# Seven value matmuls between attention's transposes, and layer 2's start moved by one folding step

## The chip, the cores and the metric

One Trainium2 chip, one core of it. The metric is the device time of one execution of the whole program in microseconds (us), the median of several runs. The kernel before takes 3842.15 us, the median of 3 runs that lie between 3840.6 and 3842.97 us. All arithmetic is in 32-bit floats.

## What is computed

The reference is a chain of four layers on a tensor `x` of 2 images, 512 channels and 32 x 32 positions. Layer 0 is a deformable attention with a position bias made by a small network, and a two-layer MLP behind it. Layer 1 is a depthwise-separable convolution whose result steers a deformable 3 x 3 convolution (9 taps, each a weighted sum of four gathered neighbours) and a gate. The change touches the seams behind layer 1, so layers 2 and 3 are what has to be seen:

```python
# layer 2: linear attention, one map per image (d = 64, N = 1024 positions)
Q, K, V = wq @ xf + bq, wk @ xf + bk, wv @ xf + bv
Qf, Kf = delu(Q).T, delu(K)               # delu(x) = 10*relu(x) + exp(10*min(x, 0))
KV = einsum('bmn,bcn->bmc', Kf, V)
norm = 1.0 / einsum('bnd,bd->bn', Qf, Kf.sum(-1) + 1e-10)
x = x + gamma * einsum('bnd,bdc,bn->bcn', Qf, KV, norm)

# layer 3: group norm (32 groups), 8-head softmax attention, output projection
h = group_norm(x) * scale + bias
q, k, v = split(W_qkv.T @ h + b_qkv)      # per head, 64 channels
attn = softmax(q @ k.T / 8, axis=-1)      # 1024 x 1024 per head
out = x + W_out.T @ (attn @ v) + b_out
```

## The kernel before

The two images go through the layers one behind the other, and the kernel weaves the end of one piece of work into the start of the next. The order of TensorE's instructions is the order in which the Python text emits them (`manual_schedule(engines={PE})`); the other engines' orders are worked out by the framework's scheduler from dependences and emission order. So the text is written as generators: each `yield` ends one small portion of matmuls, and the caller decides which generator gives its next portion.

Two seams matter here.

**Seam one: the folding of the second image and layer 2 of the first (in `layers`, L434 to L467).** The deformable convolution's nine weight taps are first multiplied with the pointwise weights of the image ("folding", `Folded.run`, L1415 on). That is 18 steps, two to a tap, each of four matmuls (L1430) and a copy (L1437) on ScalarE (ACT). The tap's 1 MB of weights is loaded by `load1` on the SyncE (SP) queue: an even tap in one transfer (L416), an odd one in two halves (L421). The loop `for i, _ in enumerate(folding)` adds something behind each folding step. From step 2 on that is one portion of `gate_image` (the gate that ends layer 1 of image 0). When the gate says `"gated"`, in step 10, layer 2 of image 0 can begin: `Linear(net, ctx2, side="right")` issues its loads, `wqk` (0.5 MB), `wv` (1 MB) and a bias row, and `aside` becomes the chain of `linear.run(0, ...)` and the group norm's terms. From step 11 on, `next(aside)` adds one of its portions behind each folding step. The first portion is `pqk` of the first half image (L1647, four matmuls), which needs `wqk` and the gated `x`. What is left of `aside` behind step 17 is taken one portion at a time behind each step of the deformable convolution of image 1 (`Deform.run`, L1508 on: four transposes `pt` L1520, then eight matmuls `po` L1552). When `aside` is done, `Attention` is made and loads its weights.

**Seam two: the end of layer 2 of image 1 and the start of attention (end of `layers`, `layer3`, `Attention.heads`).** The values of image 0, `att.values(0, turn)`, are 8 tiles of 128 positions; each tile is four accumulating matmuls (`pv3`, L1883) in one PSUM bank and one eviction by VectorE (DVE, L1892). A portion is one matmul, so there are 32. `BESIDE` says how many of them go behind each portion of layer 2 of image 1; it sums to 19. The other 13 are emitted at the beginning of `heads` as one block:

```python
ahead = [self.exponentials(*part) for part in logits(*work[0])]
for e in ahead:
    self.divide(*e)
for _ in first:
    pass
```

`heads` then runs 64 steps, half of them for each image. Step `at` works on one pair of heads and 128 query rows. On TensorE it emits the logits of the step that follows (`pl`, L1973), half of the weighting of an earlier pair of steps (`po3`, L1988; there is none in steps 0 and 1, because the first pair is only complete behind step 1), and four groups of four transposes (`pt3`, L2025), `g` = 0 to 3. The maxima of the new logits are DVE's (`m`, L2063), the exponentials ACT's (`e`, L2071), the division DVE's (L2075, L2076). The transposes of group 1 are evicted by DVE (L2034), those of groups 0, 2 and 3 by ACT (L2036), and the exponentials of the second head are held behind the eviction of group 0 (`issue_after`). The tag `pt3` has two PSUM buffers. Behind each group stands the `fill` list, pairs of (attention steps, generator, portions): the portions are spread evenly over four slots to a step. Before, the list begins with image 1's group norm terms and normalization over steps 0 to 3 (10 portions, hardly any TensorE work), image 1's 32 value matmuls over steps 4 to 15, and then its queries and keys. These value matmuls use a bank of their own (`spare`), while the rest of image 0's values take their bank from `turn`, which at that point is `pt3`: `banks["turn"] = att.ps_t, "pt3"`.

Of the kernel before, what the change touches and what calls it, by code (L numbers as in the profile page):

```python
# [3 lines left out]

# [1 line left out]

# [244 lines left out]
def chain(*parts):  # L251
    for part in parts:
        yield from part
# [6 lines left out]
def some(generator, steps):  # L260
    for _ in range(steps):
        next(generator, None)
# [14 lines left out]
def layers(net, out):  # L277
# [12 lines left out]
    with ExitStack() as later:  # L290
# [12 lines left out]
        with ExitStack() as l0a:  # L303
# [9 lines left out]
            first = net.pool(l0a, "cpb_ab", 4)  # L313
# [78 lines left out]
        with ExitStack() as l1:  # L392
            ps_m = net.psum(l1, "l1_m", 3)
            held = net.bank(l1, "l1_held")
            banks["turn"] = net.psum(l1, "l1_y", 2), "turn"
            ps_o = net.psum(l1, "l1_po", 2)

            def bank(name):
                return ps_m.tile([128, 512], F32, name=name, tag="bank")

            def po_bank(name):
                return ps_o.tile([128, 512], F32, name=name, tag="po")

            own1, image1 = ExitStack(), ExitStack()
            acc_a, acc_b = net.pool(own1, "df_acc_a"), net.pool(own1, "df_acc_b")
            tmp = net.pool(own1, "df_tmp", 1)
            f1 = Features(net, 1, own1, dram)

            f1.room = acc_b, "dfacc"

            def load1(k):
                if k % 2 == 0:
                    t = acc_b.tile([128, CC, C], F32, name="dc_w_t", tag="dfacc")
                    nc.sync.dma_start(out=t, in_=net.ins["dc_w"][:, k, :, :])  # L416
                    return [t[:, cc, :] for cc in range(CC)]
                parts = []
                for u in range(2):
                    t = got1.tile([128, 2, C], F32, name="dc_w_t", tag="got")  # L420
                    nc.sync.dma_start(out=t, in_=net.ins["dc_w"][:, k, 2 * u : 2 * u + 2, :])  # L421
                    parts += [t[:, 0, :], t[:, 1, :]]
                return parts

            accs.append(acc_a)
            deform0.buffers(image0, 3, 1, 0, side="right")
            deform0.turn, deform0.po, deform0.on_scalar = turn, po_bank, True
            found = f1.run(own1, bank, held, True)
            for i, _ in enumerate(taken):
                some(found, BOTH[i])  # L430
            image0.close()
            gate = gate_image(net, f0, deform0.acc, tmp, bank)
            for _ in range(2):
                some(found, 2)  # L434
                next(gate)

            next(found)
            folded1 = Folded(net, image1)
            got1 = net.pool(image1, "df_got_w", 2)
            first_w = load1(0)  # L440
            deform1 = Deform(net, f1, folded1, [acc_b, acc_a])
            deform1.on_scalar = True
            deform1.buffers(image1, 4, 2, 2)
            folding = folded1.run(f1, turn, load1, first_w)
            ctx2, aside, att = None, None, None
            next(gate)
            some(found, 3)
            for i, _ in enumerate(folding):
                if i < 6:
                    next(found, None)  # L450
                    next(found, None) if i % 2 else None
                if i == 6:
                    some(found, 99)
                    deform1.fetch()
                if i > 1 and aside is None and next(gate) == "gated":
                    own0.close()
                    ctx2 = ExitStack()
                    linear = Linear(net, ctx2, side="right")
                    linear.open(ctx2, side="right")
                    aside = chain(  # L460
                        linear.run(0, bank, held), group_norm_terms(net, linear.tmp, 0, bank)
                    )
                elif aside is not None:
                    next(aside)
                if i > 8:
                    deform1.prime()

            deform1.free["got"].extend([got1] * 2)
            gate = gate_image(net, f1, deform1.acc, tmp, bank)
            for i, _ in enumerate(deform1.run(turn, po_bank)):  # L470
                if att is None and next(aside, "done") == "done":
                    ctx2.close()
                    att = Attention(net, later, side="right")
                if i in range(22, 34, 2):
                    next(gate)
            image1.close()

            att.open_first(later, side="right")
            for _ in att.normalize(0):
                pass  # L480
            keys = chain(*(att.queries_keys(0, hp, turn) for hp in range(CC)))
            for _ in gate:
                some(keys, 5)
            own1.close()
            with ExitStack() as ctx:
                linear = Linear(net, ctx)
                att.open_values(later, side="right")
                linear.open(ctx)
                some(keys, 12)
                values = att.values(0, turn)  # L490
                for i, _ in enumerate(linear.run(1, bank, held)):
                    some(keys, 2)
                    some(values, BESIDE[i])
                some(keys, 99)
        layer3(net, att, later, values, banks, out)


# [7 lines left out]


BESIDE = (1, 2, 1, 1, 1, 1, 1, 1, 1, 1, 3, 3, 1, 1, 0, 0)


def first_layer(net, pool, feat, p, q):  # L510
# [932 lines left out]
class Deform:  # L1443
# [40 lines left out]
    def sum(self):  # L1484

        nc = self.net.nc
        while self.begun < self.PAIRS and self.free["sum"] and len(self.got) > 1:
            pool, t = self.new("sum", [128, 2, 256])
            for q in range(2):
                c, k = self.parts[2 * self.begun + q]  # L1490
                gpool, g = self.got.popleft()
                for s in range(4):
                    w = self.f.wts[:, c, k, s : s + 1]
                    if s == 0 and self.on_scalar:
                        nc.scalar.activation(t[:, q, :], g[:, 0, :], AF.Copy, scale=w)  # L1495
                    elif s == 0:
                        nc.vector.tensor_scalar(t[:, q, :], g[:, 0, :], w, None, ALU.mult)
                    else:
                        nc.vector.scalar_tensor_tensor(  # L1499
                            t[:, q, :], g[:, s, :], w, t[:, q, :], ALU.mult, ALU.add  # L1500
                        )
                self.free["got"].append(gpool)
            self.sums.append((pool, t))
            self.begun += 1
            self.fetch()
# [576 lines left out]
def layer3(net, att, ctx, values, banks, out):  # L2082


    att.open_heads(ctx)
    ps_f = net.psum(ctx, "l3_fill", 1)

    def spare(name):
        return ps_f.tile([128, 512], F32, name=name, tag="fill")

    first = [(0, hp, s0) for hp in range(CC) for s0 in range(0, HW, 128)]
    second = [
        (1, hp, begin + s0)
        for begin, size in ((0, 512), (512, 256), (768, 256))
        for hp in range(CC)
        for s0 in range(0, size, 128)
    ]

    def output(b, s0, size):
        if (b, s0) == (0, 0):  # L2100
            att.load_out()
        return att.project(b, s0, size, out, spare)

    def late(b, s0, size):
        yield from output(b, s0, size)

    fill = [
        (4, chain(group_norm_terms(net, att.small, 1, spare), att.normalize(1)), 10),
        (12, att.values(1, spare), 32),
        (7, att.queries_keys(1, 0, spare), 16),  # L2110
        (7, att.queries_keys(1, 1, spare), 16),
        (6, att.queries_keys(1, 2, spare), 16),
        (6, att.queries_keys(1, 3, spare), 16),
        (5, late(0, 0, 512), 16),
        (6, late(0, 512, 512), 16),
        (5, late(1, 0, 512), 16),
        (6, late(1, 512, 256), 16),
    ]
    banks["turn"] = att.ps_t, "pt3"
    att.heads(first + second, values, fill)  # L2120
    for _ in att.project(1, 768, 256, out, att.last_bank):
        pass


def program(tc, ins, out, vec_at, cst_at):
    with ExitStack() as ctx:
        net = Net(ctx, tc, ins, vec_at, cst_at)
        layers(net, out)
# [20 lines left out]
```

## Time and profile before

One execution was profiled. Its span is the time between the first and the last instruction seen.

| what | value |
|---|---|
| median of 3 runs | 3842.15 us (3840.6 to 3842.97) |
| the profiled execution's own time | 3841.13 us |
| its span | 3839.4 us |
| TensorE (PE) busy in the span | 3734.6 us (97%) |
| DVE, ACT, POOL busy | 2765.1, 2566.8, 188.2 us |
| mean DMA traffic | 44 GB/s |
| mean TensorE clock granted | 0.99 |
| position of seam one | about 2980 to 3045 us |
| position of seam two | about 3285 to 3450 us |

How to read it: 1.7 us of the execution's own time lie outside the span. TensorE's idle time, 104.8 us, is the difference of the span and its busy time. In a timeline a row is a run of equal instructions; its first number is the start in us from the span's start, its second the length, and what stands in brackets is the idle time of the engine before it and what ended that. A 128x512 matmul in 32-bit floats appears as two records in a timeline, so a folding step or one `pqk` portion is "x8" and one value matmul "x2". In a table of stretches the column `PEclk` is the share of TensorE's clock pulses that was granted.

### The profile page before, as it was taken

The page shows a single profiled execution, that of the slowest core. Times are in us where ns is not written, and L with a number is a line of the kernel's source. Part 1 is how long each engine was busy: PE and PEld are TensorE (multiplying, and loading weights), DVE is VectorE, ACT ScalarE, POOL GpSimd, SP SyncE. Part 2 cuts the span into 40 slices and gives each one's busy share as a digit, 9 for nine tenths or more (in the row PEclk, how much of TensorE's full clock was granted, in tenths as well). Part 3 has the DMA queues.
Part 4 walks back from the last instruction along what each step waited for, and adds up shares of the span by engine and source line. Part 5 has one row for each costly group of instructions (what it writes and reads, how often), then busy time and mean ns, then how long its engine had stood idle before and what let it go on. Part 6 is the DMA issues. An engine that isn't in the chain of part 4 may idle for free. (4 is left out here: it accounts for less than half of the span.)

```text
span 3839.4 us, 59395 instructions
## 1 busy us (share of the span) xinstructions
PE 3734.6 (97%) x25356; PEld 1492.3 (39%) x25356; DVE 2765.1 (72%) x3242; ACT 2566.8 (67%) x2941; POOL 188.2 (5%) x180
## 2 busy tenths in 40 slices
PE   7999999999999999999999899999979999899999
PEld 4532222223222322232233444444434544455555
DVE  6999999999999999999999310510475482566565
ACT  7999999999999999999999211211123243345544
POOL 0000000000000000000000000000252150000000
PEclk9999999999999999999999999999989999999999
DMA  3000000000000000000010000022455471000000
GB/s 111 1 23 23 23 1 23 23 23 12 12 23 23 21 3 23 23 23 1 23 56 29 33 0 1 18 82 77 134 173 187 144 273 48 1 12 1 1 20 25
DMA packets 54459, 168.57 MB, mean 44 GB/s; under 512 B 4804, under 2 KB 10436, under 8 KB 51252
## 3 DMA queue, kind: packets, MB, share of 16 engines
q1 hardware_dynamic: 31556, 83.77, 6.3%
q0 software_dynamic: 21776, 79.14, 6.2%
q8 instruction: 200, 3.28, 0.4%
q10 hardware_dynamic: 864, 1.86, 0.1%
q14 instruction: 63, 0.52, 0.0%
HBM read 156.11 MB, written 8.65 MB: 43 GB/s over the span
## 5 line engine op out<-in xcount | busy, mean ns | idle before, releaser
L888 PE MATMUL ph<-h,w_t 128*32 128x512 f32 x16384 | 1796.8, 593 | 14.0 <-ACT lo L898 6.5
L868 DVE TENSOR_TENSOR h<-ab 128x1024 f32<-128x1024 f32 x1024 | 1206.0, 1219 | 73.2 <-PE ph L888 72.2
L888 PEld LDWEIGHTS ph<-h,w_t 128*32 128x32 f32 x16384 | 548.7, 110 | 1235.5 <-issue 1031.2
L877 ACT ACTIVATE h<-h 128x1024 f32<-128x1024 f32 x832 | 869.6, 1065 | 44.4 <-DVE h L868 40.6
L901 DVE SCALAR_TENSOR_TENSOR hi<-lo,low_w,hi 128x1024 f32<-128x1024 f32 x512 | 655.0, 1279 | 27.4 <-ACT hi L900 26.8
L900 ACT ACTIVATE hi<-ph,size_b,size 128x1024 f32<-128x1024 f32 x512 | 620.5, 1212 | 15.5 <-PE ph L888 10.1
L898 ACT ACTIVATE lo<-ph,vec_t 128x1024 f32<-128x1024 f32 x512 | 571.1, 1116 | 3.8 <-PE ph L888 3.8
L2071 ACT ACTIVATE e<-pl,m 128x1024 f32<-128x1024 f32 x128 | 143.6, 1122 | 228.1 <-DVE m L2063 228.1
L1552 PE MATMUL po<-fold,turned 128*128 128x512 f32 x576 | 269.7, 612 | 3.1 <-DVE dfacc L1560 2.9
L2063 DVE TENSOR_REDUCE m<-pl 128x1 f32<-128x1024 f32 x128 | 150.8, 1220 | 144.4 <-PE pl L1973 144.4
L1120 ACT ACTIVATE h<-ph,vec_t 128x512 f32<-128x512 f32 x64 | 44.0, 687 | 310.9 <-PE ph L1112 310.4
L909 PE MATMUL sim<-hi,w 128*32 128x512 f32 x2048 | 246.1, 592 | 0.6 <-DVE hi L901 0.6
L1112 PE MATMUL ph<-xn,room 128*128 128x512 f32 x512 | 230.2, 593 | 0.0
L1101 PE MATMUL acc<-h,mlp_w_t 128*128 128x512 f32 x512 | 229.8, 592 | 0.0
L1499 DVE SCALAR_TENSOR_TENSOR sum<-got,wts,sum 128x256 f32<-128x256 f32 x432 | 184.4, 479 | 48.1 <-ACT sum L1495 45.7
L1475 POOL DMA_INDIRECT got<-table,idx x144 | 174.0, 1209 | 550.4 <-DVE sum L1499 272.1
L2025 PE MATMUL pt<-cst_t,e 128*128 128x128 f32 x1024 | 148.2, 278 | 6.5 <-ACT aT L2036 3.9
L2025 PEld LDWEIGHTS pt<-cst_t,e 128*128 128x128 f32 x1024 | 117.9, 141 | 93.2 <-issue 61.0
L1552 PEld LDWEIGHTS po<-fold,turned 128*128 128x128 f32 x576 | 107.8, 197 | 114.8 <-issue 109.7
L1101 PEld LDWEIGHTS acc<-h,mlp_w_t 128*128 128x128 f32 x512 | 97.3, 190 | 122.5 <-issue 122.0
L1112 PEld LDWEIGHTS ph<-xn,room 128*128 128x128 f32 x512 | 96.2, 190 | 117.2 <-issue 116.6
L1526 ACT COPY turned<-pt 128x512 f32<-128x512 f32 x72 | 41.9, 582 | 145.9 <-PE pt L1520 145.7
(250 smaller groups left out, 2712.1 us busy)
## 6 DMA issues: line engine op xcount, KB each, us to landing
ab<-feat_d SPq DMA_DIRECT2D x64, 512.0 KB, 3.8
room<-in_dc_w_dram SPq DMA_DIRECT2D x9, 1024.0 KB, 4.7
dc_w_t<-in_dc_w_dram SPq DMA_DIRECT2D x5, 1024.0 KB, 4.8
room<-in_mlp_w_dram SPq DMA_DIRECT2D x1, 4096.0 KB
mlp_w_t<-in_mlp_w_dram SPq DMA_DIRECT2D x1, 4096.0 KB, 13.4
dc_w_t<-in_dc_w_dram SPq DMA_DIRECT2D x8, 512.0 KB, 5.1
w_qkv_t<-in_w_qkv_dram SPq DMA_DIRECT2D x3, 1024.0 KB, 8.9
out_dram<-x_all SPq DMA_DIRECT2D x12, 256.0 KB, 2.0
```

What stands on the lines that cost most here:

```text
L868: nc.vector.tensor_tensor(h1.rearrange("p (y x) -> p y x", x=32), at_x[:, k : k + 1, :].to_broadcast([128, 32, 32]), at_y[:, k, :].unsquee ...
L877: nc.scalar.activation(h1, h1, AF.Relu)
L888: nc.tensor.matmul(ph[32 * t : 32 * t + 32, half(n)], lhsT=w2[:, c0 : c0 + 32], rhs=pair[t // 2][:, half(n)], start=True, stop=True, skip_ ...
L898: nc.scalar.activation(lo, phs[0], AF.Relu, bias=b2_lo)
L900: nc.scalar.activation(hi, phs[1], AF.Relu, bias=size_b, scale=size)
L901: nc.vector.scalar_tensor_tensor(hi, lo, low_w, hi, ALU.mult, ALU.add)
L909: nc.tensor.matmul(sim[32 * t : 32 * t + 32, half(n)], lhsT=w3[:, 30 - j : 62 - j], rhs=sums[t][:, half(n)], start=(j == 0), stop=(j == 30 ...
L1101: nc.tensor.matmul(accs[oc], lhsT=self.w2[:, m, 128 * oc : 128 * oc + 128], rhs=hs[m], start=(m == 0), stop=(m == 15),)
L1112: nc.tensor.matmul(ph, lhsT=self.w1[:, k, 128 * m : 128 * m + 128], rhs=xn[:, k, :], start=(k == 0), stop=(k == CC - 1),)
L1499: nc.vector.scalar_tensor_tensor(t[:, q, :], g[:, s, :], w, t[:, q, :], ALU.mult, ALU.add)
L1552: nc.tensor.matmul(self.out, lhsT=turned[:, at : at + 128], rhs=self.folded.w[k][:, i, :], start=(k == 0 and i == 0), stop=(k == 8 and i = ...
L2025: nc.tensor.transpose(pt[:, 128 * c : 128 * c + 128], e[:, 128 * k : 128 * k + 128], ident)
```

## The change

Two edits. In seam one a single empty portion is put ahead of layer 2 of image 0 (`iter((None,))`), so that its first `pqk` and everything of `aside` behind it is emitted one folding step (later on: one deformable step) later. The loads of `Linear` stay where they are.

In seam two the 13 leftover value matmuls (`LEFT`) are split. `BEHIND` = 6 of them stay in the block ahead of attention's step 0: the last one of tile 4, all four of tile 5, the first one of tile 6. The other 7 become the first entry of `fill`, over steps 0 and 1: none behind group 0 of step 0 and one behind each of the seven groups after it. Image 1's group norm entry thereby moves from steps 0 to 3 to steps 2 to 5, and its 32 value matmuls from 12 steps (4 to 15) to 10 (6 to 15). From step 16 on nothing is changed. The number of instructions is the same.

```diff
+from itertools import islice
...
                     linear.open(ctx2, side="right")
+
                     aside = chain(
+                        iter((None,)),
                         linear.run(0, bank, held), group_norm_terms(net, linear.tmp, 0, bank)
                     )
...
 BESIDE = (1, 2, 1, 1, 1, 1, 1, 1, 1, 1, 3, 3, 1, 1, 0, 0)
+
+
+LEFT = 32 - sum(BESIDE)
+BEHIND = LEFT - 7
...
     fill = [
+        (2, values, LEFT - BEHIND),
         (4, chain(group_norm_terms(net, att.small, 1, spare), att.normalize(1)), 10),
-        (12, att.values(1, spare), 32),
+        (10, att.values(1, spare), 32),
         (7, att.queries_keys(1, 0, spare), 16),
...
-    att.heads(first + second, values, fill)
+    att.heads(first + second, islice(values, BEHIND), fill)
```

## Prediction, made before the changed kernel ran

> **What bounds the kernel now.** I read the page's busy times first, then TensorE's list of waits, then the timeline and short stretches at the two seams.
>
> ```profile
> PE 3734.6 (97%) x25356; PEld 1492.3 (39%) x25356; DVE 2765.1 (72%) x3242; ACT 2566.8 (67%) x2941; POOL 188.2 (5%) x180
> ```
>
> TensorE is the bound, and the change removes none of its work. It can only win idle time, 104.8 us in the whole span, or time at a reduced clock. TensorE's waits, longest first, show how little of that lies at the seams (us in total, times, longest):
>
> ```profile
> PE pv L1883 <- DVE v L1892: 4.3, 5, 2.3
> ...
> PE pt L2025 <- ACT aT L2036: 3.9, 2, 2.0
> PE pqk L1647 <- DMA wqk_t<-in_wqk_dram: 3.8, 1, 3.8
> ...
> PE pt L2025 <- DVE aT L2034: 2.5, 2, 2.1
> ```
>
> Seam one is one wait of 3.8 us. The timeline, and two stretches of it, with the granted clock as the third number from the right:
>
> ```profile
> 2988.91 0.33 SPq L217 DMA_DIRECT2D wqk_t<-in_wqk_dram  x1
> ...
> 2993.52 5.29 PE L1647 MATMUL pqk<-x_all,wqk_t 128*128 128x512 f32 x8 [3.75 <-DMA wqk_t<-in_wqk_dram]
> ...
> 2998.65 3.60 PE L1430 MATMUL pw<-dc_w_t,pw_n_t 128*128 128x512 f32 x8
> ...
> 3002.08 3.60 PE L1647 MATMUL pqk<-x_all,wqk_t 128*128 128x512 f32 x8
> ```
>
> ```profile
> 2989.80:2993.40 3.60, 0.00 (x0) 0.00 (x0) 0.00 (x0) 1.87 (x2) 0.00 (x0) 1.00 0.96 331
> 2993.40:2996.80 3.40, 3.28 (x4) 1.52 (x5) 0.00 (x0) 0.00 (x0) 0.00 (x0) 0.50 0.97 355
> ```
>
> The idle stretch is followed by 3.4 us at half clock: `pqk` takes 5.29 us there and 3.60 the next time. So the wait costs 3.75 + 1.69 = 5.4 us.
>
> Seam two, TensorE alone:
>
> ```profile
> 3300.82 12.12 PE L1883 MATMUL pv<-w_qkv_t,h 128*128 128x512 f32 x24 [2.26 <-DVE v L1892]
> 3312.87 1.99 PE L1973 MATMUL pl<-qk 64*128 64x512 f32 x8
> 3314.79 1.09 PE L2025 MATMUL pt<-cst_t,e 128*128 128x128 f32 x8
> 3317.89 1.10 PE L2025 MATMUL pt<-cst_t,e 128*128 128x128 f32 x8 [2.00 <-ACT aT L2036]
> 3318.91 2.06 PE L1973 MATMUL pl<-qk 64*128 64x512 f32 x8
> 3320.90 1.09 PE L2025 MATMUL pt<-cst_t,e 128*128 128x128 f32 x8
> 3323.92 1.50 PE L2025 MATMUL pt<-cst_t,e 128*128 128x128 f32 x8 [1.93 <-ACT aT L2036]
> ```
>
> Steps 0 and 1 idle 2.00 and 1.93 us each: groups 0 and 1 take both `pt3` buffers, and group 2 waits for ACT's copy of group 0. That copy stands on ACT behind the exponential of new logits, which stands behind their maximum: from the start of `pl` at 3312.87 the maxima start at +2.02, the exponential at +3.28, the copy ends at +4.97. From 3345 on TensorE waits for nothing over 0.6 us.
>
> **Seam one, step by step.** The extra empty portion puts the folding step that is at 2998.65 ahead of the first `pqk`. Its weights (even tap, one 1 MB load) were issued at 2982.05; such loads land in a median of 4.8 us, so they are there by about 2987. TensorE is free at about 2989.6, the step takes 3.44 us beside others (8 records of 0.43), to 2993.05. `wqk`, issued at 2988.91, lands at 2993.38 (4.48 us in the chain of waits), so `pqk` starts at about 2993.5 as before, now at full clock because 0.4 us of idle time are left: to 2996.95. Before, the two were done at 3002.08. **Gain 5.1 us.**
>
> What moves with it: on SP and POOL nothing changes place. The last tap's load waits for the buffer of the folding step, which now ends 8 us sooner, and is used 6 us sooner. Attention's weights are issued one deformable step later than at 3103.81 and first used behind 3186. The second image's deformable convolution starts with one layer-2 portion less ahead of it, so its sums of gathered rows are due sooner. Third pair, the tightest: its sum is complete 4.1 us behind the first transposes now (3031.06, 3035.2), and will be needed 7.8 us behind them. DVE is busy 13 to 20 of every 20 us at 3040 to 3180 and TensorE waits for it nowhere; I take 0, with 2 us as the other end (a wait of the size of the slack at the fourth pair, 3042.3 to 3044.29). Without this cover nothing of the 5.1 would come home.
>
> **Seam two, step by step.** The wait of 2.26 us ahead of tile 5 stays (same maxima ahead of the same eviction). Then 10 instead of 24 records, and step 0 begins 14 x 0.43 = 6.0 us sooner. The point is what tile 6 does: it is begun in the block and finished behind group 3 of step 0, so it holds one `pt3` buffer all through step 0, and tile 7 holds one through step 1. In the changed kernel's emitted order group 1 therefore waits for ACT's copy of group 0, group 2 for DVE's copy of group 1, group 3 for ACT's: **the transposes go through one buffer**. From the start P of `pl`, with the offsets above:
>
> - step 0: `pl` to 1.92, group 0 to 2.47, then idle to 5.01 (copy at 4.97): 2.54 us. Group 1 to 5.56, value matmul to 6.42; DVE, which now divides first (to 5.5), has copied group 1 by about 6.35. Group 2 to 6.97, value to 7.83, group 3 to 8.38, value to 9.24. Three values are 2.58 us, so the rest is 6.66 against 6.04 now: **+0.6**.
> - step 1: one value matmul lies ahead of group 1's wait, idle falls to 1.7 us; 9.24 less four values (3.44) is 5.80, against 6.66 less 0.36 (`pm`, which moves away) less 0.4 (clock) = 5.90: **-0.1**.
>
> The seven matmuls stand nearly all behind the wait and do not fill it. Then image 1's group norm and values come two steps later: steps 2 and 3 have logits, weighting and transposes alone, without fill. Step 2 now is the nearest row: it idles 0.20 and 0.34 us. Two more such steps cost 2 x 0.54 = **+1.1**; the ends are 0 and the 2.11 us of step 3, where normalization stands in DVE's way, so 0 to +4.2. Steps 4 and 5 inherit today's 2 and 3. Steps 6 to 15 have 3.2 values a step instead of 2.7 and are bound by TensorE's work, as now. Sum of seam two: **+1.6**.
>
> **Clock.** Here a row and a rule part. The stretch 3297.15 to 3300.57 has 2.0 us idle and is followed by 3.4 us at 0.50; so are the ones with 1.93 and 2.11; the one with 1.77 of its 3.45 us idle (3314.2 to 3317.65) is not. The Trainium skill, "TensorE: Matmul & The Clock Gate", Part 1, says that half clock follows a whole idle window of about 3.4 us, and under "HAM oscillation" it advises contiguous matmuls to stay warm, which speaks against breaking up a block. By the rule as written none of the gaps of seam two costs clock and the sum is +1.6 on either side. By the rows each gap of 1.9 or more can cost 1.7: now three do (2.26, 1.93, 2.11), and afterwards 2.26, 2.54 and 2.11 can, while 1.7 lies below. I follow the rows: three for three, 0, with one spell (1.7) either way, since the windows run freely and the seam moves against them.
>
> **Sum.** -5.1 + 1.6 = -3.5. Against the profiled execution's own 3841.13 that is 3837.6. The median of the runs is 1.0 above it, so I forecast **3838.6**, its own range 3835.5 to 3842.
>
> **Rivals.**
> - *The values fill the gaps.* If the other buffer comes free, or the copies come sooner, both step gaps (3.93) vanish and one clock spell with them (1.7): 3842.15 - 5.1 - 3.9 - 1.7 + 1.1 = **3832.5**. For it: 7 x 0.86 us of work lie in just these steps. Against it: the buffer's holder and the chain of maximum, exponential, copy, which the values do not shorten. 0.17.
> - *The single buffer costs more than seam one brings (the slower side).* Every group 1 to 3 of both steps waits behind the exponentials (about 4.4 a step, 8.7 for 3.9 now: +4.8), the emptier stretches bring two more half-clock spells (+3.4), the two unfilled steps cost step 3's price (+4.2): +12.4 - 5.1 = +7.3, **3849.5**. It decides from +5.1 in seam two on. For it: 2.54 of a window of 3.4 idle in step 0. Against it: a value matmul of 0.86 covers each later copy of 0.6 to 0.7. 0.16.
> - *Seam one gives nothing.* `wqk` lands no sooner and the 5 us come back as a wait for gathered sums: 3842.15 + 1.6 = **3843.7**. For it: DMA is 0.94 busy at 3100 to 3120. Against it: no wait there now. 0.11.
>
> **Chances.** Forecast 0.56. 0.2% is 7.7 us, about what a measurement of this kernel can tell from no change: faster is below 3834.5 (nearly all of the first rival, a little of the forecast, 0.18), slower above 3849.8 (half of the second rival and a trace of the third, 0.09), within it 0.73. The range 3831 to 3847 holds the forecast, the first and third rival and the lower part of the second.
>
> **What would show it.** In the changed profile: `pqk` at about 3.6 us with at most 0.5 us of wait (right), a wait for a sum (L1499) behind 3020 (seam one given back). In step 0 a gap of about 2.5 us between group 0 and group 1 put down to ACT's copy (right); no gap over 1 us in steps 0 and 1 would prove the single buffer wrong. Gaps over 1 us in steps 2 and 3 would mean that I priced the unfilled steps too low.

## The result, and the profile after

The changed kernel takes 3837.68 us, the median of 12 runs (3833.46 to 3840.63); beside them the kernel before takes 3842.16 us (12 runs, 3839.74 to 3846.77). The two medians lie 4.5 us apart. The recorded ratio, which is not simply that of the medians, is 0.9984 with a 95% interval of 0.9977 to 0.9991: 6.1 us less, between 3.5 and 8.8. Taken again in two later groups of runs, the ratio was 0.9987 (0.9978 to 0.9995) and 0.9984 (0.9975 to 0.9993). So the gain is real in that none of the three intervals reaches 1. All three middle values are below the 7.7 us that the prediction took as the bound of "no change", though each interval reaches beyond it.

The profiled execution of the changed kernel took 3837.99 us, its span is 3836.2 us. Its busy times, from the page; the line numbers of both seams are 7 higher than before:

```profile
PE 3735.0 (97%) x25356; PEld 1488.7 (39%) x25356; DVE 2765.9 (72%) x3242; ACT 2565.7 (67%) x2941; POOL 186.2 (5%) x180
```

TensorE has the same 25,356 matmuls and the same busy time within 0.4 us. Of its waits (us in total, times, longest) those at the seams are now:

```profile
PE pt L2032 <- ACT aT L2043: 4.8, 5, 2.4
...
PE pv L1890 <- DVE v L1899: 3.3, 3, 2.3
PE pt L2032 <- DVE aT L2041: 3.0, 4, 2.2
...
PE pqk L1654 <- DMA wqk_t<-in_wqk_dram: 0.5, 1, 0.5
```

The 3.8 us wait for `wqk` has shrunk to 0.5; the wait ahead of tile 5 (2.3) stands; the transposes wait longer for ACT's copies than before (4.8 for 3.9). TensorE's timeline at seam one:

```profile
2989.36 7.03 PE L1437 MATMUL pw<-dc_w_t,pw_n_t 128*128 128x512 f32 x16
2996.90 3.67 PE L1654 MATMUL pqk<-x_all,wqk_t 128*128 128x512 f32 x8 [0.51 <-DMA wqk_t<-in_wqk_dram]
3000.41 3.60 PE L1437 MATMUL pw<-dc_w_t,pw_n_t 128*128 128x512 f32 x8
```

Two folding steps stand back to back (x16), and `pqk` runs at full clock behind them. From the first of these steps to the start of the one behind `pqk` the changed kernel takes 3000.41 - 2989.36 = 11.05 us; before, the same work, two folding steps and one `pqk`, ended at 3002.08 after starting at 2986.17: 15.91. Seam one gives 4.9 us. Seam two, steps 0 to 2 of attention:

```profile
3299.56 6.25 PE L1890 MATMUL pv<-w_qkv_t,h 128*128 128x512 f32 x10 [2.26 <-DVE v L1899]
3305.75 1.99 PE L1980 MATMUL pl<-qk 64*128 64x512 f32 x8
3307.66 0.66 PE L2032 MATMUL pt<-cst_t,e 128*128 128x128 f32 x4
3310.76 0.66 PE L2032 MATMUL pt<-cst_t,e 128*128 128x128 f32 x4 [2.44 <-ACT aT L2043]
3311.25 1.02 PE L1890 MATMUL pv<-w_qkv_t,h 128*128 128x512 f32 x2
...
3314.98 1.99 PE L1980 MATMUL pl<-qk 64*128 64x512 f32 x8
...
3319.99 0.66 PE L2032 MATMUL pt<-cst_t,e 128*128 128x128 f32 x4 [1.58 <-ACT aT L2043]
...
3324.20 1.99 PE L1980 MATMUL pl<-qk 64*128 64x512 f32 x8
...
3329.33 0.66 PE L2032 MATMUL pt<-cst_t,e 128*128 128x128 f32 x4 [0.24 <-ACT aT L2043]
3330.32 0.66 PE L2032 MATMUL pt<-cst_t,e 128*128 128x128 f32 x4 [0.34 <-DVE aT L2041]
```

Group 0 is now a single row of four transposes: group 1 no longer starts with it, but 2.44 us later, behind ACT's copy. The value matmul stands behind that gap, not in it. Steps 0 and 1 take 9.23 and 9.22 us from logits to logits.

Where the profiled time went, stretch by stretch: the changed kernel comes to seam one 3.2 us later than before (2989.36 for 2986.17), in work that the change does not touch; seam one gives back 4.9; between the seams 0.4 is lost; from the logits ahead of step 0 to those that step 16 emits (3294.26 to 3438.94, against 3295.52 to 3442.06) it gains 1.9; behind that both take 397.3. Together -3.1 us, as the two executions differ. The stretches that hold the change thus gave 4.9 - 0.4 + 1.9 = 6.4 us in this pair of profiles; the 3.2 us lost ahead of them show how far two executions can differ for other reasons. The stretch from the logits ahead of step 0 to those that step 16 emits is called the **attention stretch** below; the next table has it for all experiments.

### The profile page after: what moved, and what is told of

Its sections match the earlier page's. It is cut to its first block, busy times and chain, and to the rows that moved or that the text cites. A ratio compares the mean times of both kernels' runs of the same rounds, so it can differ in the third digit from the quotient of the medians.

```text
span 3836.2 us, 59390 instructions
## 1 busy us (share of the span) xinstructions
PE 3735.0 (97%) x25356; PEld 1488.7 (39%) x25356; DVE 2765.9 (72%) x3242; ACT 2565.7 (67%) x2941; POOL 186.2 (5%) x180
```

## The experiments

Eight new kernels and four repeats ran, in three groups, each on another chip and with its own runs of the kernel before (medians 3842.64, 3843.47 and 3842.92 us); the ratios in the table are to these, so totals of different groups are compared by their ratios. The table's first two rows are the runs of the result. They differ in the order of matmuls, in buffers and in the place of one load.

**Each seam alone, a bank of its own, and matmuls in the gap.** The first takes only `iter((None,))`; the second leaves only that out. The third gives tiles 6 and 7 the bank of `spare`, so that no open tile holds a `pt3` buffer. The fourth is seam one with the old fill list, and with tiles 6 and 7 whole between the logits and group 0 of steps 0 and 1. The third against the changed kernel:

```diff
-    att.heads(first + second, islice(values, BEHIND), fill)
+    def block():
+        for i, _ in enumerate(islice(values, BEHIND)):
+            if i == 4:
+                banks["turn"] = ps_f, "fill"
+            yield
+    att.heads(first + second, block(), fill)
```

and the fourth, against the kernel before with `iter((None,))`; what it hands to `heads` is drawn where the first steps have no weighting:

```diff
-    banks["turn"] = att.ps_t, "pt3"
-    att.heads(first + second, values, fill)
+    banks["turn"] = ps_f, "fill"
+    def tiles():
+        for _ in range(2):
+            some(values, 4)
+            yield
+    att.heads(first + second, islice(values, 5), fill, tiles())
```

> Only the empty portion ahead of layer 2 of image 0; attention's start as before. My theory (the whole gain is seam one): pqk at about 3.6 us with at most 0.5 us of wait ahead of it, 4.5 to 5.1 us won, total about 3837, ratio to before 0.9987; steps 0 and 1 idle 2.00 and 1.93 us as before. Rival (the gain came from seam two and its clock): total within 1 us of before, because the 5 us come back as waits for gathered sums (DVE L1499) behind 3020 us.

> Only the seven value matmuls between the transposes and the shifted list; seam one as before. My theory: a wait of 3.75 us and half clock at the first pqk stay; step 0 9.2 us with a gap of 2.4, step 1 9.2 us with a gap of 1.6, steps 2 and 3 idle 0.5 to 0.6 us each; from the first logits to those of step 17 143.0 us plus 1.7 for each half-clock spell (before: 141.4 plus 1.7 for each); total 1.6 us over before where the spells are the same in number, 3840 to 3844. Rival (seam two brings the gain): total about 3837.

> The changed kernel with tiles 6 and 7 of the values in the spare bank instead of pt3, nothing else. My theory (the open value tile takes one of the two pt3 buffers): groups 0 and 1 run one behind the other again, the gap moves behind group 1 and shrinks to about 1.1 us in step 0 and 0.3 us in step 1; both steps take about 7.8 us instead of 9.2, 2.8 us less than the changed kernel in all, total about 3835. Rival (the buffer is not it, the chain of maximum, exponential and copy alone sets the step): both steps stay at 9.0 us or more and the total stays at about 3837.7.

> Seam one as changed; at seam two the list of before, and the leftover values in the spare bank, tile 4's last and tile 5 ahead of step 0, the whole of tile 6 between logits and group 0 of step 0, the whole of tile 7 at the same place in step 1. My theory (work must stand between logits and group 0, and must hold no pt3 buffer): no gap over 0.3 us in steps 0 and 1, each about 7.9 us with four values; no wait of 2.26 us ahead of tile 5, because its bank is not tile 4's; from the first logits to those of step 17 136 us plus 1.7 for each half-clock spell, and at most one spell; total 3829 to 3833, below both kernels. Rival (the chain of maxima and exponentials decides, wherever values stand): steps at 9 us, total about 3837.

A half-clock spell is one stretch of 3.41 us with a granted clock of 0.50; all that overlap the attention stretch are counted.

| kernel | us, median (runs) | ratio to before, 95% | attention stretch, us | half-clock spells in it |
|---|---|---|---|---|
| before | 3842.16 (12) | | 146.54 | 3 |
| changed | 3837.68 (12) | 0.9984 (0.9977 to 0.9991) | 144.68 | 1 |
| seam one alone | 3838.81 (13) | 0.9991 (0.9983 to 1.0000) | 147.89 | 4 |
| seam two alone | 3842.05 (13) | 0.9999 (0.9990 to 1.0007) | 144.52 | 1 |
| changed, tiles 6, 7 in a bank of their own | 3834.40 (21) | 0.9980 (0.9973 to 0.9986) | 141.73 | 1 |
| seam one, tiles 6, 7 in the gap | 3829.66 (6) | 0.9971 (0.9959 to 0.9983) | 135.93 | 0 |
| changed, fill list unmoved | 3838.57 (10) | 0.9985 (0.9976 to 0.9994) | 143.57 | 1 |
| changed, two empty portions | 3839.64 (10) | 0.9985 (0.9976 to 0.9994) | 146.06 | 3 |
| changed, again | 3838.63 (12) | 0.9987 (0.9978 to 0.9995) | 144.69 | 1 |
| tiles 6, 7 in the gap, again | 3828.15 (5) | 0.9967 (0.9955 to 0.9980) | 135.93 | 0 |
| the same, two empty portions | 3830.69 (6) | 0.9967 (0.9955 to 0.9979) | 139.24 | 2 |
| changed, `wv` later | 3837.79 (11) | 0.9989 (0.9980 to 0.9998) | 144.05 | 1 |
| changed, `wv` later, again | 3836.20 (11) | 0.9984 (0.9975 to 0.9993) | 146.00 | 2 |
| changed, a third time | 3836.28 (11) | 0.9984 (0.9975 to 0.9993) | 143.92 | 1 |

The runs point to seam one: alone the seams give -3.5 us (0.9991) and -0.4 us (0.9999), each with some 3 us to either side. Seam one's interval just reaches no change and the two intervals overlap, so by the totals alone the split is likely and not shown. The profiles show it by place. In its profile seam one alone has `pqk` at 3.67 us with 0.18 us of wait, and steps 0 and 1 keep the old gaps of 2.00 and 1.92. Seam two alone keeps the wait for `wqk` (3.73 us, `pqk` 5.24) and has the new gaps (2.44 and 1.57), and steps 2 and 3 idle 0.58 us each. The first `pqk` with seam one alone and then with seam two alone:

```profile
2996.07 3.67 PE L1648 MATMUL pqk<-x_all,wqk_t 128*128 128x512 f32 x8 [0.18 <-DMA wqk_t<-in_wqk_dram]
```

```profile
2992.54 5.24 PE L1653 MATMUL pqk<-x_all,wqk_t 128*128 128x512 f32 x8 [3.73 <-DMA wqk_t<-in_wqk_dram]
```

In these two kernels every gap goes with its own edit.

The bank of its own decides whether the single buffer is the cause of the new gap. Its timeline, step 0:

```profile
3302.02 1.99 PE L1980 MATMUL pl<-qk 64*128 64x512 f32 x8
3303.93 1.09 PE L2032 MATMUL pt<-cst_t,e 128*128 128x128 f32 x8
3304.86 1.02 PE L1890 MATMUL pv<-w_qkv_t,h 128*128 128x512 f32 x2
3307.03 0.66 PE L2032 MATMUL pt<-cst_t,e 128*128 128x128 f32 x4 [1.14 <-ACT aT L2043]
...
3309.77 1.99 PE L1980 MATMUL pl<-qk 64*128 64x512 f32 x8
```

Groups 0 and 1 run together again (x8), the first value matmul comes ahead of the wait, and the gap falls from 2.44 to 1.14 us; in step 1 it falls from 1.58 to 0.28. The steps take 7.75 and 7.76 us instead of 9.23 and 9.22, and the stretch 2.95 us less at the same number of spells. So the open value tile's hold on a `pt3` buffer costs 3.0 us of the stretch, shown by taking the hold away alone.

The fourth kernel puts whole tiles where TensorE would wait. Its timeline:

```profile
3295.16 4.56 PE L1885 MATMUL pv<-w_qkv_t,h 128*128 128x512 f32 x10
3299.65 1.99 PE L1975 MATMUL pl<-qk 64*128 64x512 f32 x8
3301.57 3.70 PE L1885 MATMUL pv<-w_qkv_t,h 128*128 128x512 f32 x8
3305.10 1.04 PE L2026 MATMUL pt<-cst_t,e 128*128 128x128 f32 x8
3306.43 1.15 PE L2026 MATMUL pt<-cst_t,e 128*128 128x128 f32 x8 [0.29 <-ACT aT L2037]
3307.51 2.01 PE L1975 MATMUL pl<-qk 64*128 64x512 f32 x8
```

The 2.26 us wait ahead of tile 5 is gone (tile 5 has a free bank, so tile 4's eviction is not waited for), the copy of group 0 is waited for 0.29 us instead of 2.44, and no spell of half clock is left in the stretch: 135.93 us, 8.75 less than the changed kernel, in both executions. This version also has the old fill list, so the 8.75 us are not the place of the tiles alone. At 0.9971 and 0.9967 it is faster than the kernel before. In the group in which it ran beside the changed kernel its median is 10.5 us lower (3828.15 of 5 runs against 3838.63 of 12), so it beats that one too, by an amount that so few runs leave wide: its five runs spread from 3827.21 to 3835.54.

**The unfilled steps, the load's landing, and repeats.** One kernel keeps the fill list of before and draws the seven matmuls beside it; one puts two empty portions ahead of layer 2 (the last two lines of the diff); the changed kernel and the best version ran again.

```diff
-        (2, values, LEFT - BEHIND),
...
-        (10, att.values(1, spare), 32),
+        (12, att.values(1, spare), 32),
...
+                if 0 < 4 * at + g < 8:
+                    next(beside, None)
...
-                        iter((None,)),
+                        iter((None, None)),
```

> The changed kernel, the seven value matmuls at the same places and in the same bank, but image 1's group norm terms and values at the steps where they were before (0 to 3 and 4 to 15). My theory (the shift of that list costs two unfilled steps of about 0.55 us idle each): steps 0 and 1 stay at 9.2 us with gaps of 2.4 and 1.6; from the first logits to those of step 17 about 141.9 us plus 1.7 for each half-clock spell, 1.1 less than the changed kernel's 143.0; total within the noise of the changed kernel, about 1 us below it. Rival (the shift costs nothing, because the later steps have more work to fill with): 143.0 plus 1.7 for each spell.

> The changed kernel with two empty portions instead of one. My theory (seam one is a race of one folding step with a load of 4.5 us): the wait of 0.2 to 0.5 us ahead of pqk goes, nothing else is won, total 0 to 0.5 us below the changed kernel, so no difference that can be measured. Rival (layer 2 still comes too early, or now too late): over 2 us either way, as a new wait behind 3020 us.

> The changed kernel once more, beside the version with whole tiles in the gap, for a comparison on one chip. My theory: 3836 to 3840; step 0 and 1 at 9.2 us as in its first profile; whether the gap of 2.4 us in step 0 is followed by half clock depends on how the clock's windows of 3.41 us cut it, so 0 or 1 spells of 1.7 us there. Rival (the gap never costs clock): no spell there in any profile, which one more profile can't settle.

> The version with seam one as changed and whole value tiles between logits and group 0, again. My theory: 3828 to 3832, 6 to 9 us below the changed kernel on the same chip; from the first logits to those of step 17 135.9 us with 0 or 1 spell. Rival (its first runs, few in number, were lucky): within 3 us of the changed kernel.

With the list unmoved the stretch is 143.57 us with one spell, 1.1 us below the changed kernel's with one spell: what the two more unfilled steps were priced at. It idles 0.34 and 2.11 us in steps 2 and 3, as the kernel before. Its total, 3838.57, does not tell it from the changed kernel.

The repeat of the changed kernel shows the same steps (9.23 us, gaps of 2.44 and 1.58) but another seam one. The load is issued on SP's queue at 2985.52, while the two folding steps run:

```profile
2982.79 7.03 PE L1437 MATMUL pw<-dc_w_t,pw_n_t 128*128 128x512 f32 x16
...
2992.88 5.26 PE L1654 MATMUL pqk<-x_all,wqk_t 128*128 128x512 f32 x8 [3.06 <-DMA wqk_t<-in_wqk_dram]
```

Here `pqk` starts 7.4 us behind the issue, and 3.06 us of wait and the half clock are back, although the extra folding step is there. The kernel with the list unmoved shows the same (3.23 us of wait, 7.5 us behind the issue). In the other six profiles with one empty portion and the loads unmoved `pqk` starts 4.5 to 5.0 us behind it. In the repeat the stretch that took 15.91 us before takes 15.19 (2982.79 to 2997.98), where the first profile of the changed kernel has 11.05. So the gain of seam one depends on a landing time that varies, and in two of eight profiled executions most of it was lost.

With two empty portions `pqk` starts 7.6 us behind the issue and does not wait for `wqk`; that would just cover the long landing, but whether this execution had one its trace does not tell. Everything behind is due sooner by another step. The timeline near 3130, where the gathered rows are weighted and summed on ACT and DVE:

```profile
3130.24 3.60 PE L1559 MATMUL po<-fold,turned 128*128 128x512 f32 x8
3136.63 1.09 PE L1527 MATMUL pt<-cst_t,sum 128*128 128x128 f32 x4 [2.79 <-DVE sum L1506]
3137.51 4.78 PE L1559 MATMUL po<-fold,turned 128*128 128x512 f32 x8
```

A wait of 2.79 us for a sum appears, and the stretch behind it is at half clock (4.78 us instead of 3.60). The total, 3839.64, is no better than with one empty portion.

**What sets the landing, and the best version with more cover.** One kernel is the version with the tiles in the gap and two empty portions. One holds the 1 MB load of `wv` until the first `pqk` is evicted, by a one-column copy into its buffer; it ran twice, beside the changed kernel:

```diff
-        self.wqk, self.wv = net.load("wqk", w), net.load("wv", w)
-        self.bv = net.load_row("bv_row", w)
+        self.w, self.wqk, self.wv = w, net.load("wqk", w), None
...
             qk.append(qf)
+            if self.wv is None:
+                src = net.ins["wv"]
+                self.wv = self.w.tile(list(src.shape), F32, name="wv_t", tag="wv")
+                nc.vector.tensor_copy(self.wv[:, 0, :1], qf[:, :1])
+                nc.sync.dma_start(out=self.wv, in_=src)
+                self.bv = net.load_row("bv_row", self.w)
```

> The version with whole value tiles between logits and group 0 (3828.2 and 3829.7 us in two looks), with a second empty portion ahead of layer 2. Theory (the load of wqk lands 4.5 us behind its issue in some executions and 7.4 us in others, and two empty portions cover both): the wait for wqk is 0 and pqk 3.6 us, and the median of the runs is 0 to 2 us below the version with one empty portion, 3826 to 3830. Rival (one portion more only makes the gathered sums of the deformable convolution due sooner, as in the run with two empty portions, which showed one wait of 2.8 us): the median is 1 to 3 us above it, 3829 to 3832, with a wait for a sum over 1 us behind 3000.

> The changed kernel, with layer 2's load of wv (1 MB) held until the first pqk has been evicted, so that behind wqk's issue only half a tap of weights (0.5 MB) and a bias row share the DMA engines. Theory (wqk is slowed by what is issued right behind it): wqk is there in clearly less than the 4.5 us seen so far, about 3.5 us, so pqk waits for nothing and takes 3.6 us, and no landing of 7 us is seen; the total is that of the changed kernel or up to 2 us less, 3836 to 3839. Rival (the landing time is wqk's own, or is set by what was issued ahead of it): 4.5 us as before, or 7.4 us in about 2 of 7 looks.

> The kernel with the later load of wv once more, for a second landing of wqk. Theory: about 3.5 us from issue to the start of pqk or earlier, no wait, as in the first look, and the same total within 1 us. Rival: one of the two looks shows a landing of 4.5 or 7.4 us.

> The changed kernel beside the two runs with the later load of wv, on the same chip. Theory of the shared load: wqk lands 4.5 us or more behind its issue (4.5 to 4.8, or 7.4), pqk waits 0.2 to 0.7 us, or 3.1 us with half a clock behind it; total 3838 to 3839. Rival: its landing is no later than in the two runs with the later load.

The second empty portion brings nothing here either: 3830.69 us and 0.9967, the ratio of the version without it. There is a wait of 2.0 us for a sum, and the stretch behind it is at half clock:

```profile
3119.16 0.97 PE L1522 MATMUL pt<-cst_t,sum 128*128 128x128 f32 x4 [1.97 <-DVE sum L1501]
3120.26 5.02 PE L1554 MATMUL po<-fold,turned 128*128 128x512 f32 x8
```

In this execution `wqk` landed 4.4 us behind its issue, so one empty portion would have done. The rival of that run had the wait and the median right; by the ratio the second portion costs nothing that can be told.

The theory that `wqk` is slowed by the load issued right behind it fell. In the first of the two kernels, SP's queue first and then TensorE:

```profile
2989.02 0.33 SPq L218 DMA_DIRECT2D wqk_t<-in_wqk_dram  x1
...
3001.07 0.42 SPq L1669 DMA_DIRECT2D wv_t<-in_wv_dram  x1
```

```profile
2986.29 7.03 PE L1437 MATMUL pw<-dc_w_t,pw_n_t 128*128 128x512 f32 x16
2993.56 3.67 PE L1653 MATMUL pqk<-x_all,wqk_t 128*128 128x512 f32 x8 [0.24 <-DMA wqk_t<-in_wqk_dram]
```

The load of `wv` is issued 12 us later, and `pqk` still waits for `wqk`: it starts 4.5 us behind the issue, 4.7 in the second run of this kernel, against 4.8 in the changed kernel beside them. I had expected about 3.5. What makes the landing 7.4 us in some executions stays open: neither of the two profiles showed one, but at two in eight that says little. The DMA engines as a whole were hardly slower in the two late profiles: in the 4.5 us behind the issue they moved 277 and 279 GB/s, against 285 to 299 in the other six. One rival is untested: the load of half a tap (0.5 MB) is issued 0.8 us ahead of `wqk` in every run, none of it has moved by then (0 GB/s in the 2 us before), and so the two share the engines. That half tap and the one behind `wqk` were left where they are in all runs.

## Why the prediction was right, point by point

The forecast was 3838.6 us; 3837.68 was measured. The sum of -3.5 us lies at the edge of the interval of the ratio (-8.8 to -3.5), and its terms did not all come as they were written. The mechanisms of both seams were right. That the total came within 1 us is in part luck: where the prediction had -5.1, +1.6 and 0 for the clock, the first profile of the changed kernel has -4.5 from seam one to seam two, about +1.5 and about -3.4, and executions with a late landing take back part of it.

- **Seam one, 5.1 us.** The mechanism is as predicted: `pqk` takes 3.67 us with 0.51 of wait, and the stretch is 4.9 us shorter in the profile of the changed kernel. What the step took as fixed, a landing at 4.48 us, holds in six of eight profiles; in the other two 3.1 to 3.2 us of wait and a spell come back. And the term taken as 0, with 2 us as the other end, the sums that are due sooner, was 0, 1.4 and 2.1 us in the three profiles of the changed kernel. In the two that have these waits, they stand near 3117 and 3138 us, not at the third and fourth pair near 3031 to 3044 that the prediction took as the tightest. So 5.1 is the gain of a good execution, not of each.
- **The single buffer, step 0 +0.6 and step 1 -0.1.** Predicted 9.24 us for each step, measured 9.23 and 9.22; predicted gaps 2.54 and 1.7, measured 2.44 and 1.58, put down to ACT's copy. The bank of its own shows the cause. The rival in which the values fill the gaps fell in the changed kernel; it is what the two rearranged versions then do, one in part and one nearly whole.
- **Two unfilled steps, +1.1.** Predicted 0.54 us of idle time in each of steps 2 and 3; measured 0.58 and 0.58. The kernel with the list unmoved is 1.1 us shorter in this stretch. The end of +4.2 did not come.
- **Clock, 0 with one spell either way.** This is the term that was mis-sized. Seam two has three half-clock spells before and one after; I had counted three for three. If a spell is put at the prediction's 1.7 us, the stretch without them is 141.4 us before and 143.0 after: +1.5, near the predicted sum of seam two of 1.6; with them it is -1.9. In the three profiles of the changed kernel the count was one each time, but not always the same spell; the old order of seam two was profiled twice, with three spells and, with seam one alone, four. That this makes up for seam one's late landings in the medians fits the totals, but the totals alone cannot separate the two.
- **The rival in which the single buffer costs more than seam one brings** decides from +5.1 us in seam two on. Seam two alone came at 0.9999 of before (0.9990 to 1.0007), which is at most 2.7 us slower: it fell. **The rival in which seam one gives nothing** fell for the changed kernel as a whole, but its mechanism, waits for gathered sums, is real: with the second empty portion it takes 2.0 and 2.8 us.

On the rule and the row: the rows came nearer than the rule, since no window of seam two was wholly idle and spells came all the same. But counting gaps by their length, as the prediction did, gave the wrong number: the gap of 2.44 us stands in eight of the profiles and only two have a half-clock spell that sets in near its end. What decides is how it lies in the windows. The unmoved list has the same 2.44 us gap in step 0 as the changed kernel, but in it the gap lies inside one window of 3.41 us. Two windows each, as rows of stretches: start and end, length, then busy time (and instructions) of TensorE, its weight loads, DVE, ACT and POOL, then the granted clock, the DMA share and GB/s. First with the list unmoved:

```profile
3307.80:3311.21 3.41, 0.97 (x7) 0.45 (x5) 2.84 (x4) 1.76 (x4) 0.00 (x0) 1.00 0.00 0
3311.21:3314.62 3.41, 3.41 (x10) 2.22 (x11) 1.95 (x4) 1.03 (x2) 0.00 (x0) 0.50 0.00 0
```

and then in the changed kernel:

```profile
3306.50:3309.91 3.41, 1.82 (x10) 0.61 (x6) 2.14 (x2) 0.89 (x1) 0.00 (x0) 1.00 0.00 0
3309.91:3313.33 3.42, 2.57 (x12) 1.38 (x12) 2.64 (x6) 2.34 (x6) 0.00 (x0) 1.00 0.00 0
```

With 2.44 of 3.41 us idle the next window has half clock, and step 0 takes 10.76 us; with the gap cut into 1.59 and 0.85 by a window's boundary nothing follows, and it takes 9.23. A whole idle window, as the Trainium skill has it ("TensorE: Matmul & The Clock Gate", Part 1), is not needed; but the gap's length alone does not tell either. The page's advice under "HAM oscillation", which the prediction held against breaking up a block, stands there for a loop that waits for a DMA behind each short run of matmuls, so it does not decide this case.

## What to carry to other kernels

Work that is to fill a wait must come ahead of the waiting instruction in the engine's order, and its buffer must not be the one that the wait is for: seven matmuls behind the wait, on a shared buffer, lengthened the step, and the same kind of matmuls ahead of it in a bank of their own took away nearly all the idle time. A load that is covered to within half a microsecond is covered in some executions only; but more cover also makes all that follows due sooner, so look for the next thing that will be late before adding it. And where single gaps of about 2 us decide over half-clock spells, compare stretches with the spells counted, or the clock hides the size of the change.

## What was not expected of the hardware

- **Idle windows.** In the 14 profiles, between 2600 and 3825 us, all the windows of 3.41 us with 2.04 us or more of idle TensorE time (89, those in a chain of spells among them) were followed by one at half clock. From 1.87 to 2.01 us both occur. Below that, 120 of the 126 full-clock windows with 0.9 us or more were not followed by one; the other six (1.14 to 1.74 us idle) all begin at 3287 to 3291 us, around the narrow matmuls ahead of attention. The other eight profiles have windows of 0.90 to 1.34 us idle beginning at 3286 to 3294 us, and none was followed. What sets the six apart was not tried.
- **The landing of one load.** The same 0.5 MB load, issued in the same order among the same neighbours, let `pqk` start 4.5 to 5.0 us behind its issue in six profiles and 7.4 to 7.5 us in two. Taking 1 MB away behind it did not shorten the 4.5, and the engines' total rate was within a tenth in all eight. The cause is open.
